# A Restormer block on one core: the first image's normalisation scaled on VectorE from PSUM, a shorter attention step, and a new order of the instructions

## The chip, the core and the metric

The kernel runs on one core of one Trainium2 chip, in fp32 throughout. The metric is the device time of one launch in microseconds, median of several runs. TensorE (PE), VectorE (DVE), ScalarE (ACT), GpSimd (POOL) and SyncE (SP) each take their own instructions strictly in the order in which the program holds them, and wait for each other through semaphores; DMA transfers are issued from the queues of SP and POOL (and at the start ACT).

## The reference, cut to what matters

```python
B, C, H, W = 16, 128, 96, 96; HEADS = 8; HID = 4 * C
xn1 = layernorm(x over C)                                  # LN1
q, k, v = xn1 @ wq.T, xn1 @ wk.T, xn1 @ wv.T               # per pixel
q, k = l2norm over the 9216 pixels, per channel
attn = softmax(einsum('bhcn,bhdn->bhcd', q, k) * D**-0.5)  # 16x16 for each of 8 heads
x = x + (attn @ v) @ wp.T
xn2 = layernorm(x over C)                                  # LN2
h1 = einsum('bchw,oc->bohw', xn2, w_in)                    # 128 -> 512 channels
h2 = depthwise 3x3 convolution of h1
x = x + einsum('bchw,oc->bohw', gelu(h2), w_out)           # 512 -> 128 channels
```

## The kernel before

**Tiling.** An image is 128 channels (the partitions) by 96 rows of 96 pixels. It is worked in 8 bands of 12 rows (1152 pixels), a band in 3 units of 4 rows (384 pixels). The hidden layer's 512 channels are 4 chunks of 128. A *job* is one chunk of one band; there are 128 bands.

**Stages of an image.** `norm(i, False)` is LN1: batches of 4 x 128 pixels are transposed by TensorE into PSUM (line 708), VectorE takes statistics (bn_stats, L716), POOL works out variance (L721) and its power -1/2 (L725), the batch is scaled, and TensorE adds the scaled batch to a 128x129 Gram matrix (L758) and transposes it back to the channels' layout (L808), from where ACT copies it into the ring `xn` (L814). In all images but the first, ACT copies the transposed batch from PSUM to the SBUF tile `zT` (L745), VectorE takes the statistics from there and POOL scales it in place (L751). In the first image the batch goes through the three PSUM banks `acc` that the taps use later; ACT copies it to SBUF (into tiles `h3` that are still free), and VectorE and POOL scale one half each (L751). `attention` turns the Gram matrix into one 128x128 matrix: L2 norms of q and k from the Gram matrix (L912 to L931, small 128x2 operations), the scores (L916 to L941), the exponential on ACT (L946, PSUM to SBUF), softmax on VectorE (L951 to L954), two more matmuls, and the matrix to SBUF (L971). `norm(i, True)` applies it (`mix`, L661), adds x (L667 on VectorE for the first bands of the first image, else L670 on ACT and a DMA that adds, L673), takes LN2's statistics from PSUM, and VectorE writes the scaled result to `xn` (`place`, L812).

**The feed-forward part.** For each job TensorE computes `hidden` (L1008) into one of four PSUM banks `h`, ACT copies it to SBUF (`kept`, L1013). The depthwise convolution's nine taps are split: VectorE does most of them as scalar_tensor_tensor operations on 128x1152 (below: *taps*; the first of a job takes POOL's `merged` as its addend, L1036 with acc as output; the middle ones L1040; the last one writes `h3`, L1036 with h as output). All middle and last taps of a job read the `acc` that the tap before them wrote. Two to four taps of a job are products made by ACT (L1024), brought in by POOL (`merge`, L1027, L1030) and by DMAs that POOL issues and that add in flight (L1049, L1052). ACT then takes the GELU (L1057). For one chunk in a third of the bands TensorE does the whole convolution instead (L1120). TensorE's `out` (L1161) sums the four chunks, and VectorE adds the result to x (`add`, L1168); SP stores it.

**What sets the order.** The functions do not issue instructions; they hand operations to a planner (`Plan`) with an engine, an assumed duration, what is read and written, and a place: a number of jobs from the operation's position in the work plus the entry of its kind in the table `AT` (entries `_0` are for the first image). `RANK` is added for the choice within an engine only, not for the turn in which buffers are given out. `Plan.order` plays the program through with the assumed durations; whenever an engine is free, the ready operation with the lowest place goes. The order of these starts is the order of the instructions in the program; at run time nothing is reordered.

Of the kernel before, what the change touches and what calls it, by code (L numbers as in the profile page):

```python
# [50 lines left out]
    load_w=-10696.6, weights=-1325.7, zeros=-1188.75, load_a=-32.75, forth_a=537.05, stats_a=22,  # L51
    variance_a=-862.55, power_a=-5924.95, pool_product=152.05, merge=-5342.4, scaled_a=-5192.6, gram=1195.35,
    back_a=409.4, place_a=886.65, attention=-25.55, mix=300.55, residual=204, mixed=1426, add_x=-865.9,
    forth_b=1131.25, stats_b=0.4, variance_b=-1458.9, power_b=-5365.35, shift_b=20.9, scaled_b=-3615.05,
    back_b=417.45, place_b=-1328.4, halo=2133.65, hidden=417.15, kept=888.55, products=-29.95, add_last=-5291.25,
    tap=11.15, add_first=-5453.25, gelu=2338.65, conv=1193.95, conv_gelu=10.7, out=420.9, add=-1325.35, store=7.1,
    mix_0=137.4, residual_0=1.6, mixed_0=28.95, add_x_0=-5926.95, gram_0=299.15, forth_a_0=-996.9, forth_b_0=321.4,
    stats_a_0=6.45, stats_b_0=-501.55, scaled_a_0=-863.8, copied_a=1384.75, copied_b=1870.85, copied_a_0=86.7,
    copied_b_0=1111, scaled_b_0=-128.2, back_a_0=299.35, back_b_0=412.9, place_a_0=137.4, place_b_0=-1368.1,
    shift_b_0=22.8, late=9.7,  # L60
)
RANK = dict(tap=-712.55, products=1729.15, forth_a=-347.95, forth_b=-713.5, conv_gelu=-713.7, mix=-53.4)
# [190 lines left out]
def tile_restormer_block(  # L253
# [92 lines left out]
    ccol = const.tile([P, 2, 2], F32, name="ccol")  # L346
    ncq = const.tile([1, P], F32, name="ncq")
    wqkT = const.tile([P, 2 * P], F32, name="wqkT")
    cqk = const.tile([1, 2 * P], F32, name="cqk")
# [98 lines left out]
    def move(p, f, r, w, ns, first=0):  # L448
        op("SP", 60 + first, p, f, r, w, 900 + SLACK, dma=ns)
# [15 lines left out]
    def weights(p):  # L465
# [4 lines left out]
        def loads():  # L470
            a, b = (flat(h3_bufs[plan.slot["h3", ("weights", k)]]) for k in range(2))
            v["win"] = a[:, :HID].rearrange("p (n c) -> p n c", c=P)
            v["wout"], v["wp"] = a[:, HID : 2 * HID], a[:, 2 * HID : 2 * HID + P]
            v["wqk"], v["wqkT"] = b[:, : 2 * P], b[:, 2 * P : 4 * P]
            v["wt"] = b[:, 4 * P : 8 * P].rearrange("p (t c) -> p t c", c=P)
            v["w1centre"], v["wvT"] = b[:, :P], b[:, P : 2 * P]
# [20 lines left out]
        def keep_qkp(pt):  # L497
            nc.vector.tensor_copy(v["wqkT"], pt[:, : 2 * P])
            nc.vector.tensor_scalar(wqkT, pt[:, : 2 * P], w1, None, ALU.mult)
            nc.vector.tensor_copy(wpT, pt[:, 2 * P : 3 * P])  # L500
            nc.vector.tensor_copy(v["wvT"], pt[:, 3 * P :])
            nc.vector.tensor_scalar(v["w1centre"], centre, w1, None, ALU.mult)
# [85 lines left out]
        pc = ("h", ("weights", "centred"))  # L588
        pe(1000, at("weights", p), centred, [("w", "qk"), mine[1]], [pc])
        dve(800, at("weights", p), keep_centred, [pc], [("w", "qk")])  # L590
# [54 lines left out]
    def norm(i, second, place_of):  # L645
# [41 lines left out]
        def pixels(s, m):  # L687
# [8 lines left out]
            by_dve = QT // 2 if early else 0  # L696
            apart = i == 0 and not second

# [11 lines left out]
            def stats(j):  # L710

                if j == 0:
                    d["st"] = small.tile([P, QB * QT // 2, 6], F32, tag="st", name=f"st_{name}_{m}")
                h, k = divmod(2 * j, QT)
                of = d["pT", qs[h]] if second or DIRECT else zT(qs[h])[:, :, :P]
                nc.vector.bn_stats(d["st"][:, j, :], of[:, k : k + 2, :].rearrange("p t c -> p c t"))  # L716
# [6 lines left out]
            def power():  # L723
                rstd = d["rstd"] = rstds[m] = small.tile([P, QB * QT], F32, tag="rstd", name=f"rstd_{name}_{m}")
                nc.gpsimd.tensor_tensor(rstd, d["ve"], mhalf, ALU.pow)  # L725
# [21 lines left out]
            def scaled(engine, q, ks):  # L747
                z = zT(q)[:, ks[0] : ks[-1] + 1, :P]
                t = (q - qs[0]) * QT
                rstd = d["rstd"][:, t + ks[0] : t + ks[-1] + 1]  # L750
                engine.tensor_tensor(z, z, rstd.unsqueeze(2).to_broadcast([P, len(ks), P]), ALU.mult)  # L751
# [12 lines left out]
            for q, tr in zip(qs, trs):  # L764
                units = {t // TPU: None for t in range(q * QT, (q + 1) * QT)}
                zt = zt_of(q)
                both = [(*zt, j) for j in range(2)]
                if apart and q % 2 == 0:
                    four = [(*zt_of(k), j) for k in (q, q + 1) for j in range(2)]
                    op("POOL", 200, at("zeros", s), lambda q=q: zT(q), [], four, 300)  # L770
                if second or DIRECT:
                    pe(112 * QT, at("forth" + ab, s, i), lambda q=q: forth(q), [xtok(u) for u in units], [tr])
                    continue
                pe(112 * QT, at("forth" + ab, s, i), lambda q=q: forth(q), [xtok(u) for u in units], [tr, both[0]])
                act(t_copy(QT * P), at("copied" + ab, s, i), lambda q=q: copied(q), [tr], both)
            for j in range(QB * QT // 2):
                of = trs[2 * j // QT] if second or DIRECT else (*zt_of(qs[2 * j // QT]), 0)
# [3 lines left out]
            for h, q in enumerate(qs if not second else ()):  # L781
                zt, sh = zt_of(q), s + STEP["scaled"] * h
                if DIRECT:
# [3 lines left out]
                if by_dve:  # L787
                    dve(by_dve * 150 + 60, at("scaled" + ab, sh, i), lambda q=q: scaled(nc.vector, q, range(by_dve)), [bt], [(*zt, 0)], True)
                pool((QT - by_dve) * T_SCALED + 100, at("scaled" + ab, sh, i), lambda q=q: scaled(nc.gpsimd, q, range(by_dve, QT)), [bt], [(*zt, 1)] if by_dve else [(*zt, 0), (*zt, 1)], True)
                if True:  # L790
                    pe(QT * 228, at("gram", sh, i), lambda q=q: gram(q), [(*zt, 0), (*zt, 1), ("w", "ones")], [("g", i)])
# [59 lines left out]
    def attention(s, i):  # L851


        places_of = dict(kq="ma", em="ma", y="ma", gs="mb", e="mb", a="mb")
        columns = dict(ps_u=0, ps_r=256, ps_c=256, ps_n=384, ps_kq=0, ps_qk=128, ps_y=256, ps_m=0, ps_d=384)
# [52 lines left out]
        def _():  # L908
            pn, pc = ps([P, 2], "ps_n"), ps([P, 2], "ps_c")
# [10 lines left out]
        @step("DVE", 670)  # L920
        def _():

            n2 = sb([P, 2], "n2")
            nc.vector.tensor_mul(n2, v["ps_c"], ccol[:, 0, :])
            nc.vector.tensor_add(n2, n2, ccol[:, 1, :])
            nc.vector.tensor_add(n2, v["ps_n"], n2)
            nc.vector.tensor_scalar(n2, n2, 1e-24, None, ALU.max)

        @step("POOL", 700)
        def _():  # L930
            nc.gpsimd.tensor_tensor(sb([P, 2], "rn"), v["n2"], mhalf[:, :2], ALU.pow)  # L931

        @step("DVE", 300)
        def _():
            nc.vector.tensor_scalar(sb([P, 1], "rq"), v["rn"][:, 0:1], float(D) ** -0.5, None, ALU.mult)

            nc.vector.tensor_scalar(sb([P, P], "kq"), v["ps_kq"], v["rn"][:, 1:2], None, ALU.mult)
# [6 lines left out]
        def _():  # L944

            nc.scalar.activation(sb([P, P], "e"), v["ps_qk"], AF.Exp, scale=v["rq"])  # L946

        @step("DVE", 1060)
        def _():
            em = sb([P, P], "em")  # L950
            nc.vector.tensor_mul(em, v["e"], blocks)  # L951
# [294 lines left out]
```

## Time and profile before

| | us |
|---|---|
| median of 3 runs (lowest to highest) | 4059.35 (4056.95 to 4065.53) |
| the profiled execution | 4061.62 |
| its span | 4059.9 |
| first tap starts / last tap starts | 107.11 / 4048.15 |

The page of the profile gives each engine's busy time, the groups of instructions by line with the mean time of one, and the idle time before them with what ended it. The windows of the trace give busy time by stretch, the timeline the start of each instruction. An operation's start to the next one's start on the same engine is the time that it really costs there, since ends overlap with the following start.

### The profile page before, as it was taken

Reading aid. Unit: us, or ns where it says so; the run is one execution under the profiler, and the core shown is the slowest. Engines: PE = TensorE matmul, PEld = TensorE weight load, DVE = VectorE, ACT = ScalarE, POOL = GpSimd, SP = SyncE. Lnnn points to the kernel's source line nnn. Section 1 sums busy time; section 2 is a strip of 40 time slices with the busy share of each in tenths; the row PEclk is TensorE's granted clock in tenths of the full one; section 3 lists DMA queues with packets and bytes.
Section 4 is the critical chain, followed back from the end, with each engine's and each line's share of the span. In section 5 each row is a group of like instructions: output and inputs, shape, how many; then the busy total and the mean of one; then the engine's idle time right before and its main releaser. Section 6 shows DMA issues by size and latency. Waiting matters only on the chain. (4 is left out here: it accounts for less than half of the span.)

```text
span 4059.9 us, 50967 instructions
## 1 busy us (share of the span) xinstructions
PE 3920.2 (97%) x16758; PEld 2516.4 (62%) x16758; DVE 3878.3 (96%) x4452; ACT 3579.4 (88%) x5204; POOL 3372.2 (83%) x3109
## 2 busy tenths in 40 slices
PE   8999999999999999999999999999999999999999
PEld 6656666666666666666666666666666566656555
DVE  6999999999999999999999999999999999999998
ACT  3989988999889888999989898989998989989886
POOL 6878978888888888888888888888888878888674
PEclk9999999999999999999999999999999999999999
DMA  2889999899998999999999999999999999999996
GB/s 90 168 185 202 203 202 194 185 204 201 192 200 185 193 196 195 202 202 202 193 198 211 192 194 188 211 189 205 198 193 193 197 196 202 195 205 185 185 189 143
DMA packets 191690, 777.41 MB, mean 191 GB/s; under 512 B 22208, under 2 KB 23616, under 8 KB 191424
## 3 DMA queue, kind: packets, MB, share of 16 engines
q0 software_dynamic: 151920, 622.33, 80.9%
q1 hardware_dynamic: 38256, 151.73, 10.1%
q8 instruction: 132, 2.16, 0.2%
q14 instruction: 134, 1.10, 0.1%
q10 hardware_dynamic: 1248, 0.09, 0.0%
HBM read 148.85 MB, written 75.50 MB: 55 GB/s over the span
## 5 line engine op out<-in xcount | busy, mean ns | idle before, releaser
L1024 ACT ACTIVATE pr<-h,ratio 128x1152 f32<-128x1152 f32 x1494 | 1826.5, 1269 | 32.5 <-DMA h<-pr 13.0
L1040 DVE SCALAR_TENSOR_TENSOR acc<-h,ratio,acc 128x1152 f32<-128x1152 f32 (+1 forms) x1308 | 1809.5, 1383 | 11.4
L1027 POOL TENSOR_TENSOR merged<-pr,h 128x1152 f32<-128x1152 f32 x466 | 1220.3, 2619 | 101.1 <-DVE acc L1036 61.0
L1008 PE MATMUL h<-xn,winT 128*128 128x384 f32 (+2 forms) x2802 | 1087.6, 496 | 21.0 <-ACT h L1013 8.3
L1161 PE MATMUL h<-h,woutT 128*128 128x384 f32 x3072 | 1072.1, 489 | 11.5 <-ACT h L1013 5.5
L1120 PE MATMUL h<-xn,comp 128*128 128x380 f32 (+2 forms) x2430 | 892.1, 484 | 4.7 <-ACT h L1013 2.0
L1013 ACT COPY h<-h 128x384 f32<-128x384 f32 (+2 forms) x1401 | 652.5, 492 | 198.2 <-PE h L1008 192.9
L1161 PEld LDWEIGHTS h<-h,woutT 128*128 128x128 f32 x3072 | 566.5, 190 | 377.4 <-ACT h L1013 13.6
L1036 DVE SCALAR_TENSOR_TENSOR acc<-h,ratio,merged 128x1152 f32<-128x1152 f32 x466 | 692.6, 1486 | 28.3 <-POOL merged L1030 9.1
L1052 POOL DMA_DIRECT2D h<-pr x466 | 455.6, 978 | 307.7 <-DVE h L1036 71.6
L1008 PEld LDWEIGHTS h<-xn,winT 128*128 128x128 f32 x2802 | 489.1, 190 | 301.6 <-issue 34.5
L1057 ACT ACTIVATE h<-h,ksum 128x1152 f32<-128x1152 f32 (+1 forms) x586 | 614.2, 1076 | 62.6 <-DMA h<-pr 61.3
L1036 DVE SCALAR_TENSOR_TENSOR h<-h,ratio,acc 128x1152 f32<-128x1152 f32 x467 | 654.9, 1402 | 11.1 <-PE h L1161 6.5
L1120 PEld LDWEIGHTS h<-xn,comp 128*128 128x128 f32 x2430 | 433.9, 190 | 246.0 <-issue 19.1
L1049 POOL DMA_DIRECT2D pr<-pr x466 | 466.5, 1005 | 107.7 <-ACT pr L1024 86.0
L708 PE MATMUL h<-ident,x 128*128 128x128 f32 x2212 | 322.7, 275 | 28.7 <-DMA x<-in_x_dram 9.6
L708 PEld LDWEIGHTS h<-ident,x 128*128 128x128 f32 x2212 | 262.5, 141 | 139.6 <-issue 48.6
L725 POOL TENSOR_TENSOR rstd_b<-ve_b,mhalf 128x4 f32<-128x4 f32 x288 | 334.7, 1167 | 14.5
L751 POOL TENSOR_TENSOR zT<-zT,rstd_a 128x512 f32<-128x512 f32 x270 | 333.5, 1238 | 8.7
L725 POOL TENSOR_TENSOR rstd_a<-ve_a,mhalf 128x4 f32<-128x4 f32 x288 | 309.1, 1074 | 16.9
L661 PE MATMUL h<-xn,mwT 128*128 128x384 f32 x768 | 289.8, 495 | 8.3 <-ACT x L670 2.5
L758 PEld LDWEIGHTS g<-zT 128*128 128x128 f32 x2160 | 271.0, 191 | 41.1 <-POOL zT L751 7.0
(189 smaller groups left out, 3977.1 us busy)
## 6 DMA issues: line engine op xcount, KB each, us to landing
pr<-pr POOLq DMA_DIRECT2D x466, 576.0 KB, 7.6
h<-pr POOLq DMA_DIRECT2D x466, 576.0 KB, 7.5
x<-in_x_dram SPq DMA_DIRECT2D x128, 576.0 KB, 7.5
out_dram<-x SPq DMA_DIRECT2D x127, 576.0 KB, 4.6
x<-in_x_dram POOLq DMA_DIRECT2D x123, 576.0 KB, 8.7
out_dram<-x SPq DMA_DIRECT2D x3, 192.0 KB, 1.9
h<-in_L_conv_w_in_dram SPq DMA_DIRECT2D x1, 256.0 KB, 3.4
h<-in_L_conv_w_out_dram SPq DMA_DIRECT2D x1, 256.0 KB, 3.7
```

Source lines behind the costliest of these rows:

```text
L708: nc.tensor.transpose(d["pT", q][:, k, :], xt[:, j * P : (j + 1) * P], ident)
L725: nc.gpsimd.tensor_tensor(rstd, d["ve"], mhalf, ALU.pow)
L1008: nc.tensor.matmul(rows(ph), lhsT=winT[:, n, :], rhs=window(xn, r0 + r, e - r, 1), start=True, stop=True)
L1013: nc.scalar.copy(window(h1_, r, e - r, 1), rows(d.pop(("ph", r))))
L1024: nc.scalar.activation(to, shifted(t), AF.Copy, scale=ratio[:, n, t : t + 1])
L1027: nc.gpsimd.tensor_tensor(merged, d["pr", dma_taps[0]], shifted(UNIT), ALU.add)
L1036: nc.vector.scalar_tensor_tensor(to, shifted(t), ratio[:, n, t : t + 1], also, ALU.mult, ALU.add)
L1040: nc.vector.scalar_tensor_tensor(to, shifted(t)[:, lo:hi, cut], ratio[:, n, t : t + 1], to, ALU.mult, ALU.add)
L1049: nc.gpsimd.dma_start(out=d["pr", dma_taps[1]], in_=d["pr", t], accum_op=ALU.add)
L1057: nc.scalar.activation(h3, h3, AF.Gelu, bias=ksum[:, z, n : n + 1])
L1120: nc.tensor.matmul(d["pc"][:, lo:hi, cut], lhsT=comp[:, t, :], rhs=window(xn, r0 + dy, UR, dx)[:, lo:hi, cut], start=(t == order[0]), stop ...
L1161: nc.tensor.matmul(rows(d["po"]), lhsT=woutT[:, n, :], rhs=h3s[g, n][:, s * UR : (s + 1) * UR, :], start=(k == 0), stop=(k == NCH - 1),)
```

## The change

1. **First image, LN1.** The batch stays in its `acc` bank. VectorE takes the statistics from PSUM and, when POOL has the power, scales the whole batch from PSUM into the SBUF tile (one operation of 128x4x128 instead of one of 128x2x128 on VectorE and one on POOL). ACT's copy is gone. The bank comes free after VectorE's scaling, not after ACT's copy.
2. **Attention, all images.** The factor that was applied to the linear part of the norms by VectorE is put into a new constant `wqk2c`, so that both parts of the norm are summed in PSUM; VectorE adds the constant part in one operation (four before). The maximum with 1e-24 moves to POOL. The factor D to the power -1/2 moves from an operation on `rq` into the scaling of `kq`. The exponential is written to PSUM and masked from there.
3. **The planner's numbers**: attention's assumed durations follow these edits, a load is assumed to land after 2000 instead of 900, and the tables `AT` and `RANK` are replaced.
4. The result of the power is written over its input (`ve`); a plain renaming in the rows below.

```diff
 AT = dict(
-    load_w=-10696.6, weights=-1325.7, zeros=-1188.75, load_a=-32.75, forth_a=537.05, stats_a=22,
...
+    load_w=-2305.35, weights=639.95, zeros=-342.95, load_a=-42.4, forth_a=-588.2, stats_a=1671.35,
...
-RANK = dict(tap=-712.55, products=1729.15, forth_a=-347.95, forth_b=-713.5, conv_gelu=-713.7, mix=-53.4)
+RANK = dict(tap=-1882.15, products=-1879.1, forth_a=-433, forth_b=-526, conv_gelu=-1389, mix=-1794.75)
...
-        op("SP", 60 + first, p, f, r, w, 900 + SLACK, dma=ns)
+        op("SP", 60 + first, p, f, r, w, (2000 if w else 900) + SLACK, dma=ns)
...
-            nc.vector.tensor_scalar(ccol[:, 0, :], c, 2.0, None, ALU.mult)
-            nc.vector.scalar_tensor_tensor(ccol[:, 1, :], c, NTOK / 2.0, ccol[:, 0, :], ALU.mult, ALU.mult)
+            nc.vector.tensor_scalar(ccol, c, 1.0, None, ALU.mult)
+            nc.vector.scalar_tensor_tensor(ccol, ccol, float(NTOK), ccol, ALU.mult, ALU.mult)
+            nc.vector.tensor_tensor(wqk2c, v["ptwos"], wqkT, ALU.mult)
...
-            by_dve = QT // 2 if early else 0
             apart = i == 0 and not second
+            from_psum = second or DIRECT or apart
...
-                if DIRECT:
+                if from_psum:
                     dve(605, at("scaled" + ab, sh, i), lambda q=q: direct(q), [bt, trs[h]], [(*zt, 0), (*zt, 1)])
...
-                if by_dve:
-                    dve(by_dve * 150 + 60, at("scaled" + ab, sh, i), lambda q=q: scaled(nc.vector, q, range(by_dve)), [bt], [(*zt, 0)], True)
...
-                nc.tensor.matmul(pc[:, z : z + 1], lhsT=wqkT[:, zs], rhs=v["s"], start=True, stop=True)
-                nc.tensor.matmul(pn[:, z : z + 1], lhsT=v["prod"][:, zs], rhs=ones, start=True, stop=True)
+                nc.tensor.matmul(pn[:, z : z + 1], lhsT=wqk2c[:, zs], rhs=v["s"], start=True, stop=False)
+                nc.tensor.matmul(pn[:, z : z + 1], lhsT=v["prod"][:, zs], rhs=ones, start=False, stop=True)
...
-            nc.vector.tensor_mul(n2, v["ps_c"], ccol[:, 0, :])
-            nc.vector.tensor_add(n2, n2, ccol[:, 1, :])
-            nc.vector.tensor_add(n2, v["ps_n"], n2)
-            nc.vector.tensor_scalar(n2, n2, 1e-24, None, ALU.max)
+            nc.vector.tensor_add(sb([P, 2], "n2"), v["ps_n"], ccol)
...
+            nc.gpsimd.tensor_scalar(n2, n2, 1e-24, 1.0, ALU.max, ALU.mult)
+            nc.gpsimd.tensor_tensor(sb([P, 2], "rn"), n2, mhalf[:, :2], ALU.pow)
...
-            nc.vector.tensor_scalar(sb([P, 1], "rq"), v["rn"][:, 0:1], float(D) ** -0.5, None, ALU.mult)
-            nc.vector.tensor_scalar(sb([P, P], "kq"), v["ps_kq"], v["rn"][:, 1:2], None, ALU.mult)
+            nc.vector.tensor_scalar(
+                sb([P, P], "kq"), v["ps_kq"], v["rn"][:, 1:2], float(D) ** -0.5, ALU.mult, ALU.mult
+            )
...
-            nc.scalar.activation(sb([P, P], "e"), v["ps_qk"], AF.Exp, scale=v["rq"])
+            nc.scalar.activation(ps([P, P], "ps_e"), v["ps_qk"], AF.Exp, scale=v["rn"][:, 0:1])
...
-            nc.vector.tensor_mul(em, v["e"], blocks)
+            nc.vector.tensor_mul(em, v["ps_e"], blocks)
```

**How the order moves, at three places.** Line numbers of the changed kernel are about 2 to 8 higher (taps L1036 and L1040 become L1038 and L1042, add L1168 becomes L1170, place L812 becomes L816, statistics L716 become L724). Numbers at the end of a name are those of buffers.

The first place is VectorE in the middle of the first image's LN1 (h_... are SBUF tiles that hold batches, `st_a` the statistics of image 0). Before:

```order
L716 BN_STATS st_a_9_392<-h_6_160 128x6
L751 TENSOR_TENSOR h_4_158<-h_4_158,rstd_a_4_375 128x2x128
L716 BN_STATS st_a_9_392<-h_6_160 128x6
L716 BN_STATS st_a_10_414<-h_7_161 128x6
L716 BN_STATS st_a_11_422<-h_7_161 128x6
L716 BN_STATS st_a_10_414<-h_7_161 128x6
L551 COPY h_1_155<-h_73 128x512
L552 TENSOR_SCALAR winT<-h_73,w_99 128x512
L751 TENSOR_TENSOR h_4_158<-h_4_158,rstd_a_5_420 128x2x128
L751 TENSOR_TENSOR h_5_159<-h_5_159,rstd_a_6_434 128x2x128
```

And now, read from `acc`, whole batches:

```order
L724 BN_STATS st_a_6_342<-acc 128x6
L737 TENSOR_TENSOR h_4_159<-acc,ve_a_5_344 128x4x128
L724 BN_STATS st_a_7_371<-acc 128x6 x2
L737 TENSOR_TENSOR h_5_160<-acc,ve_a_6_363 128x4x128
L724 BN_STATS st_a_8_386<-acc 128x6 x2
L737 TENSOR_TENSOR h_5_160<-acc,ve_a_7_383 128x4x128
```

Before, statistics ran up to seven batches ahead of the scaling and the preparation of weights (L551, L552 and others) stood among them; now each scaling stands one or two batches behind its statistics, and most weight preparation comes after the Gram matrix is complete.

The second place is TensorE in the first image's attention, from the transposition of the scores (L941, now L943) to the matmul with the softmax's result (L958, now L960). `x_1`, `x_2`, `x_3` are bands of the second image. Before:

```order
L941 MATMUL h_75<-ident,kq_856 128x128
L708 MATMUL h_74<-ident,x_1_531 128x128 x2
L708 MATMUL h_74<-ident,x_2_836 128x128 x2
L708 MATMUL h_73<-ident,x_2_836 128x128 x4
L708 MATMUL h_76<-ident,x_2_836 128x128 x3
L708 MATMUL h_76<-ident,x_3_869 128x128
L958 MATMUL h_75<-wpT,a_879 128x128
```

Now, with weight preparation (L493, L576) between them:

```order
L943 MATMUL h_73<-ident,kq_725 128x128
L493 MATMUL h_76<-ident,h_1_156 128x128 x4
L716 MATMUL h_74<-ident,x_0_536 128x128
L716 MATMUL h_74<-ident,x_1_702 128x128 x3
L716 MATMUL h_75<-ident,x_1_702 128x128 x4
L576 MATMUL h_76<-comp,centre 128x512
L493 MATMUL h_74<-ident,h_1_156 128x128 x4
L960 MATMUL h_73<-wpT,a_766 128x128
```

The second image's batches have moved back (8 transpositions less stand before this attention), and the weights stand in the gaps of the attention. In the whole program TensorE has 233 matmuls ahead of the first matmul of this attention (271 in the kernel before) and 392 ahead of the first `hidden` (441).

The third place is VectorE in the middle of the program, around the norms of image 8's attention (`n_8`); the rows with `ratio` are taps. Before:

```order
L1040 SCALAR_TENSOR_TENSOR acc<-h_2_143,ratio,acc 128x1152
L924 TENSOR_TENSOR n_8_13284<-g_11959,ccol 128x2
L925 TENSOR_TENSOR n_8_13284<-n_8_13284,ccol 128x2
L926 TENSOR_TENSOR n_8_13284<-g_11959,n_8_13284 128x2
L927 TENSOR_SCALAR n_8_13284<-n_8_13284 128x2
L1036 SCALAR_TENSOR_TENSOR h_4_158<-h_2_143,ratio,acc 128x1152
L1168 TENSOR_TENSOR x_7_3_12374<-h_73,x_7_3_12374 128x384
L1036 SCALAR_TENSOR_TENSOR acc<-h_3_144,ratio,merged 128x1152
L935 TENSOR_SCALAR rq_13305<-rn_13293 128x1
L937 TENSOR_SCALAR kq_13307<-g_11959,rn_13293 128x128
```

And now:

```order
L1042 SCALAR_TENSOR_TENSOR acc<-h_2_144,ratio,acc 128x1152
L927 TENSOR_TENSOR n_8_12874<-g_11477,ccol 128x2
L1042 SCALAR_TENSOR_TENSOR acc<-h_2_144,ratio,acc 128x1152
L724 BN_STATS st_a_1_12882<-zT_164 128x6
L1042 SCALAR_TENSOR_TENSOR acc<-h_2_144,ratio,acc 128x1152
L1170 TENSOR_TENSOR x_7_3_12008<-h_73,x_7_3_12008 128x384
L1038 SCALAR_TENSOR_TENSOR h_1_156<-h_2_144,ratio,acc 128x1152
L937 TENSOR_SCALAR kq_12904<-g_11477,rn_12888 128x128
L1038 SCALAR_TENSOR_TENSOR acc<-h_3_145,ratio,merged 128x1152
```

Six small operations have become two, and single operations stand alternately with taps. Over the whole program a tap stands directly behind another tap in 390 places (549 in the kernel before); behind the first tap, two or more other operations stand between two taps in 45 places (210).

More of the change, by code (lines that the diff above doesn't have):

```diff
@@ L723, in power @@
             def power():
-                rstd = d["rstd"] = rstds[m] = small.tile([P, QB * QT], F32, tag="rstd", name=f"rstd_{name}_{m}")
-                nc.gpsimd.tensor_tensor(rstd, d["ve"], mhalf, ALU.pow)
+                rstd = d["rstd"] = rstds[m] = d["ve"]
+                nc.gpsimd.tensor_tensor(rstd, rstd, mhalf, ALU.pow)
             def direct(q):
@@ L770, in pixels @@
                     op("POOL", 200, at("zeros", s), lambda q=q: zT(q), [], four, 300)
-                if second or DIRECT:
-                    pe(112 * QT, at("forth" + ab, s, i), lambda q=q: forth(q), [xtok(u) for u in units], [tr])
+                if from_psum:
+                    to = [tr] if second or apart else [tr, both[0]]
+                    pe(112 * QT, at("forth" + ab, s, i), lambda q=q: forth(q), [xtok(u) for u in units], to)
                     continue
```

67 lines of the change are left out of this document (35 added, 32 removed).

## The prediction, made before the changed kernel ran

> **What bounds the kernel now.** First the page's totals:
>
> ```profile
> PE 3920.2 (97%) x16758; PEld 2516.4 (62%) x16758; DVE 3878.3 (96%) x4452; ACT 3579.4 (88%) x5204; POOL 3372.2 (83%) x3109
> ```
>
> Two engines are full, PE and DVE. A share over the whole span doesn't tell which one gives way, so I cut the span at the first and the last tap (the timeline of DVE) and ask for busy time by window. Columns: sum and mean of PE, PEld, DVE, ACT, POOL, then granted clock, DMA share, GB/s.
>
> ```profile
> 107.11 2.19 DVE L1036 SCALAR_TENSOR_TENSOR acc<-h,ratio,merged 128x1152 f32<-128x1152 f32 x1 [1.58 <-POOL merged L1027]
> 4048.15 1.42 DVE L1036 SCALAR_TENSOR_TENSOR h<-h,ratio,acc 128x1152 f32<-128x1152 f32 x1
> 0.00:107.10 107.10, 89.60 (x608) 73.53 (x609) 65.49 (x197) 38.75 (x80) 70.32 (x141) 0.97 0.26 86
> 107.10:4048.10 3941.00, 3822.37 (x16128) 2438.51 (x16126) 3809.67 (x4251) 3538.12 (x5119) 3301.85 (x2969) 1.00 0.93 195
> 4048.10:4059.90 11.80, 8.21 (x25) 4.33 (x24) 3.10 (x5) 2.54 (x6) 0.00 (x0) 1.00 0.14 50
> ```
>
> So time = start 107.1 + tap stretch 3941.0 + tail 11.8. In the stretch DVE is idle for 131 us (3.3%), PE for 119, at a granted clock of 1.00, and the DMA engines are at 0.93. The waits of DVE tell whom it lacks (columns: us in total, times, longest):
>
> ```profile
> DVE x L1168 <- PE h L1161: 37.4, 46, 2.9
> DVE xn L812 <- PE h L808: 20.5, 27, 1.7
> DVE st_a L716 <- ACT zT L745: 13.0, 11, 2.6
> DVE acc L1036 <- POOL merged L1030: 9.1, 13, 1.8
> DVE st_b L716 <- PE h L708: 8.9, 12, 2.6
> ```
>
> There is no large wait. PE's busy time contains pauses between queued matmuls, while DVE's operations follow each other back to back; PE's sums also wait for the taps, four chunks at a time. I take DVE as what sets the stretch: a microsecond less there shortens it by nearly one, as long as PE and the transfers follow. That is my main choice.
>
> **The change part by part.** The taps, their products, additions and transfers are the same in number; what differs is small operations and order.
>
> *Attention on VectorE.* The groups of one operation each (count | busy, mean ns | idle before), then the spread (min/median/max ns) of three of them, and the POOL group behind the spread:
>
> ```profile
> L924 DVE TENSOR_TENSOR n<-g,ccol 128x2 f32<-128x2 f32 x15 | 2.2, 145 | 0.0
> L925 DVE TENSOR_TENSOR n<-n,ccol 128x2 f32<-128x2 f32 x16 | 13.9, 870 | 0.5
> L926 DVE TENSOR_TENSOR n<-g,n 128x2 f32<-128x2 f32 x15 | 2.4, 159 | 0.5
> L927 DVE TENSOR_SCALAR n<-n 128x2 f32<-128x2 f32 x16 | 7.5, 466 | 0.6
> L935 DVE TENSOR_SCALAR rq<-rn 128x1 f32<-128x1 f32 x16 | 2.3, 146 | 0.8 <-POOL rn L931 0.8
> L937 DVE TENSOR_SCALAR kq<-g,rn 128x128 f32<-128x128 f32 x15 | 5.1, 339 | 0.0
> L951 DVE TENSOR_TENSOR em<-e,blocks 128x128 f32<-128x128 f32 x16 | 13.1, 818 | 2.3 <-ACT e L946 2.3
> L954 DVE TENSOR_SCALAR a<-em,rden 128x128 f32<-128x128 f32 x16 | 8.2, 512 | 0.6
> L925 DVE TENSOR_TENSOR n<-n,ccol x16: 160/578/3058, 63.0 to 3750.1; 128x2 f32<-128x2 f32 x16
> L927 DVE TENSOR_SCALAR n<-n x16: 169/169/2499, 63.4 to 3750.5; 128x2 f32<-128x2 f32 x16
> L951 DVE TENSOR_TENSOR em<-e,blocks x16: 274/288/2814, 66.3 to 3764.6; 128x128 f32<-128x128 f32 x16
> L1027 POOL TENSOR_TENSOR merged<-pr,h 128x1152 f32<-128x1152 f32 x466 | 1220.3, 2619 | 101.1 <-DVE acc L1036 61.0 <-ACT pr L1024 30.7 <-ACT h L1013 4.5
> ```
>
> The operations that read only SBUF (L925, L927, L951, L954) are sometimes held for up to 3 us, about one merge of POOL; those that read PSUM (L924, L926, L937) keep their 0.15 to 0.34. The change removes L924, L925, L927, L935, keeps one addition from PSUM (price of L926, as before), and lets L951 read PSUM, which I price at L937, same shape from PSUM. Saved per image: 0.145 + 0.870 + 0.466 + 0.146 + (0.818 - 0.339) = 2.11 us; 15 attentions lie in the stretch: **-31.6**. Lower bound: the holds merely move to the next operation, and only the smallest durations go, 0.145 + 0.160 + 0.169 + 0.146 = 0.62, times 15 = -9.3 (reading PSUM then gains nothing, 0.288 against 0.339). I take the means: the rows show holds at these operations, while L924 and L926, next to them, show none. ACT's exponential into PSUM and POOL's added maximum lie on engines with 12% and 17% free. The maximum takes about L721's 0.52 (below), the removed operations about as much, so the attention's own chain stays as long: nothing.
>
> [...]
>
> *The order on VectorE.* A tap behind another tap waits for it (it reads its `acc`). Timeline of DVE, start and duration ("x2" is two in a row):
>
> ```profile
> 2040.11 2.87 DVE L1040 SCALAR_TENSOR_TENSOR acc<-h,ratio,acc 128x1152 f32<-128x1152 f32 x2
> 2042.89 0.42 DVE L716 BATCH_NORM_STATS2 st_a<-zT 128x6 f32<-128x256 f32 x1
> 2043.23 1.40 DVE L1040 SCALAR_TENSOR_TENSOR acc<-h,ratio,acc 128x1152 f32<-128x1152 f32 x1
> 2044.54 0.42 DVE L716 BATCH_NORM_STATS2 st_a<-zT 128x6 f32<-128x256 f32 x1
> ```
>
> Two taps take 2042.89 - 2040.11 = 2.78, so the first of them takes 2.78 - 1.31 = 1.47 up to the next tap's start; a tap before a small operation takes 2044.54 - 2043.23 = 1.31. So a direct pair costs about 0.15 more. The rows of the order give 549 such pairs before, 390 now: 159 x 0.15 = **-24**. Bounds: 0, if the operation that now stands between pays the gap itself, and -24; I take -24, since these rows show the statistics following without it.
>
> [...]
>
> *The start.* PE's transpositions of the second image and preparations that stood ahead of the first attention have moved back. The places in the timeline:
>
> ```profile
> 27.49 1.04 PE L708 MATMUL acc<-ident,x 128*128 128x128 f32 x8
> 57.13 0.27 ACT L879 COPY gs<-g 128x129 f32<-128x129 f32 x1 [0.36 <-PE g L758]
> 99.85 2.33 PE L1008 MATMUL h<-xn,winT 128*128 128x480 f32 x6
> L708 PE MATMUL h<-ident,x 128*128 128x128 f32 x2212 | 322.7, 275 | 28.7 <-DMA x<-in_x_dram 9.6
> ```
>
> LN1 ends at 57.1, the first `hidden` comes at 99.9, the first tap at 107.1. Of 441 matmuls ahead of the first `hidden` 392 remain; 49 at 1.04 / 8 = 0.13 are 6.4. In the attention itself PE now has five matmuls more between L943 and L960, 0.65 if nothing there waits. Bounds: +0.65 (only these five count, the rest was covered by waits) to -12 (44 net at the group's mean of 0.275); I take **-6**, by the row of this stage.
>
> *Is VectorE too slow for the first image's banks?* A bank of three is now held until VectorE has scaled the batch:
>
> ```profile
> L716 DVE BATCH_NORM_STATS2 st_a<-h 128x6 f32<-128x256 f32 x36 | 13.5, 414 | 0.4 <-ACT h L745 0.4
> L721 POOL TENSOR_SCALAR ve_a<-st_a 128x4 f32<-128x4 f32 x288 | 146.3, 520 | 44.2 <-DVE st_a L716 43.9
> L725 POOL TENSOR_TENSOR rstd_a<-ve_a,mhalf 128x4 f32<-128x4 f32 x288 | 309.1, 1074 | 16.9
> L812 DVE TENSOR_TENSOR xn<-x,h 128x384 f32<-128x384 f32 x384 | 206.4, 547 | 25.3 <-PE h L808 20.5 <-ACT h L1013 1.1 <-ACT pr L1024 1.0
> L606 DVE COPY woutT<-h 128x512 f32<-128x512 f32 x1 | 0.7, 669 | 0.0
> 8.66 1.94 PE L708 MATMUL acc<-ident,x 128*128 128x128 f32 x8 [8.66 <-DMA x<-in_x_dram]
> ```
>
> Two statistics 0.83, variance 0.52, power 1.07, and the scaling, not in the trace: above L812's 0.55 with fewer elements, I take L606's 0.67. That is 3.1 us a bank; with three banks (`acc`) one batch each 1.03 us, while 18 batches between 8.7 and 57.1 come every 2.7 us by the loads. VectorE's own part, 1.5 us a batch, fits too. Both costs are covered by the loads; if they were not, 18 x 1.03 = 18.5 would still be below the 48 available. Nothing. On the other hand eight statistics of the second image, ahead of the first tap before, now lie in the stretch, at 0.34 from start to start (2043.23 - 2042.89): **+2.7**.
>
> *What is late next.* The stretch gets 31.6 + 24 - 2.7 = 53 us (1.3%) shorter, and PE, ACT and the DMA engines must do the same work in it. The DMA share of 0.93 becomes 0.943, so free DMA time falls by a fifth; PE's idle 119 us would fall to 66, by 45%. The waits of DVE, 89 us in the five rows above, won't shrink by themselves. If they grow about as much as PE's idle time falls, by 40%, that is +35; at least 0. I take the middle, **+18**.
>
> Sum: -31.6 - 24 - 6 + 2.7 + 18 = -41. The profiled execution took 4061.6 (its span 4059.9 and 1.7 around it), so 4020.7; it was 2.3 above the median of the runs, so **4018**.
>
> **The rivals.**
>
> *Better:* the waits don't grow and the start gives its 12: 4018 - 18 - 6 = 3994. For it: all engines have over 2% idle. Against: 0.93 on the DMA engines.
>
> *The alternation is worth nothing:* 4018 + 24 = 4042. For it: only a few dozen starts were read in the timeline. [...]
>
> *The holds move to the next operation:* 31.6 - 9.3 = 22 back: 4040.
>
> *The change doesn't do what it says,* VectorE doesn't set the stretch. PE is as busy (3822 against 3810) and both kernels have the same matmuls; then the stretch stays 3941 and only the start counts: 4059.3 - 6 = 4053.
>
> *Slower: an operation that waits for PE stops the taps.* VectorE takes its instructions in turn; with single operations alternating with taps, an addition (L1170) whose sum isn't ready holds the next tap, and behind it POOL's merge and PE's next sum. A wait costs 37.4 / 46 = 0.81. Two thirds of the bands, 85, have all four chunks on VectorE; one more wait in each is 85 x 0.81 = +69: 4018 + 69 = 4087. It undoes the gain from 41 / 0.81 = 51 new waits, and shows as slower from about 60. For it: waits on PE are already the largest rows. Against: an addition had single taps around it in most places before, too.
>
> **How the numbers follow.** Forecast (4005 to 4036) 0.47; better 0.13; alternation nothing 0.08; holds move 0.08; VectorE not the bound 0.10; slower 0.14. The range goes from below the better case, 3990 (it could win another 4 by fewer waits), to just above the 4053, 4056: outside are the slower case and a small part of the better one. A measurement of this kernel tells about 0.2%, 8 us, from no change. Faster than 4051.2: 0.47 + 0.13 + 0.08 + 0.08 = 0.76; the same 0.10; slower than 4067.5: 0.14.
>
> **What would show it.** Right: DVE's busy time in the stretch falls by some 50 us; n2's addition stays near 0.16 and em near 0.34 without a maximum near 3; tap to next start 1.31 in about 160 more places; the first tap near 101; DVE's waits on PE grow by less than 35. Wrong: the stretch keeps 3941 with DVE's idle time grown by what its busy time lost (VectorE was not the bound), waits of L1170 and L816 in over 100 places (slower), em's holds found again at L954's successor, or a first image whose `acc` waits for VectorE's scaling (L737) so that the Gram matrix ends after 57.

## The result, and the profile after

| | before | after |
|---|---|---|
| median (lowest to highest), us | 4059.93 (4056.95 to 4065.53) | 4014.02 (4013.62 to 4020.85) |
| ratio, 95% interval | | 0.9889 (0.9872 to 0.9906) |
| profiled execution / its span | 4061.62 / 4059.9 | 4020.85 / 4019.1 |

The change gains 1.1%, some 45 us. The forecast was 4018. The sum came out, but not the choice that it stands on: VectorE doesn't set the pace. The sections below show both. The profiled execution of the changed kernel was the slowest of its four, 6.8 us above their median (1.7 before), so the profiles show 41 us of the 45.

The totals of the page, and the windows of the trace cut at the first and the last tap (columns as before: length; busy time of PE, PEld, DVE, ACT, POOL; clock, DMA share, GB/s):

```profile
PE 3908.1 (97%) x16760; PEld 2525.4 (63%) x16760; DVE 3834.9 (95%) x4390; ACT 3562.0 (89%) x5186; POOL 3378.7 (84%) x3107
0.00:110.34 110.34, 88.18 (x556) 69.92 (x557) 67.82 (x186) 22.35 (x50) 50.84 (x113) 1.00 0.22 72
110.34:4007.40 3897.06, 3812.38 (x16184) 2451.64 (x16183) 3763.96 (x4201) 3537.74 (x5133) 3327.91 (x2995) 1.00 0.94 197
4007.40:4019.10 11.70, 7.51 (x23) 3.89 (x21) 3.08 (x4) 1.88 (x5) 0.00 (x0) 1.00 0.14 50
```

The tap stretch is 3941.0 - 3897.1 = 44 us shorter, the start 3 longer, the tail the same. In the stretch VectorE's busy time fell by 45.7 and its idle time stayed (131.3 before, 133.1 now). That reads exactly as forecast: a full engine got less to do. But another pair of numbers stands beside it: TensorE's idle time in the stretch fell from 118.6 to 84.7, and its busy time by 10, with 56 rows of matmuls more in it. One profile can't tell which engine led; it took loads put on each of them.

The attention's operations on VectorE after the change, by form, and the spread (min/median/max):

```profile
L927 DVE TENSOR_TENSOR n<-g,ccol 128x2 f32<-128x2 f32 x15 | 2.2, 145 | 0.0
L937 DVE TENSOR_SCALAR kq<-g,rn 128x128 f32<-128x128 f32 x15 | 5.2, 345 | 0.0
L953 DVE TENSOR_TENSOR em<-g,blocks 128x128 f32<-128x128 f32 x15 | 4.2, 282 | 0.0
L956 DVE TENSOR_SCALAR a<-em,rden 128x128 f32<-128x128 f32 x16 | 10.6, 662 | 0.6
L953 DVE TENSOR_TENSOR em<-g,blocks x15: 276/282/285, 249.8 to 3703.1; 128x128 f32<-128x128 f32 x15
L956 DVE TENSOR_SCALAR a<-em,rden x16: 285/288/2034, 76.4 to 3704.0; 128x128 f32<-128x128 f32 x16
```

What reads PSUM is not held: the mask (em), now read from there, takes 276 to 285 ns, where it went up to 2814. Part of the hold has moved to `a`, which reads only SBUF: 662 on average, 512 before. The two operations between them, `den` and `rden`, read only SBUF too and are not held (286 and 164 ns on average, before and after).

TensorE's own waits, which the prediction doesn't show. Of before, then of after (us in total, times, longest):

```profile
PE h L808 <- POOL rstd_b L725: 14.9, 14, 2.6
PE h L708 <- DMA x<-in_x_dram: 9.6, 10, 2.2
PE acc L708 <- DMA x<-in_x_dram: 8.7, 1, 8.7
PE h L1008 <- ACT h L1013: 8.3, 10, 2.6
PE g L958 <- DVE a L954: 7.3, 7, 2.2
```

```profile
PE h L1010 <- ACT h L1015: 11.6, 14, 3.3
PE h L812 <- POOL ve_b L733: 9.1, 11, 1.6
PE h L1122 <- ACT h L1015: 6.0, 8, 1.9
PE acc L716 <- DVE st_a L724: 5.5, 12, 1.0
PE h L716 <- DMA x<-in_x_dram: 1.5, 3, 0.8
```

The ten waits for loaded images (9.6 us) became three (1.5), those for the LN2 power (`rstd_b`, now `ve_b`) fell from 14.9 to 9.1. There is also a new one: in the first image TensorE waits twelve times for VectorE before it fills an `acc` bank (L716 <- `st_a`).

### The profile page after: what moved, and what is told of

It reads as the page before. It is cut to its first block, busy times and chain, and to the rows that moved or that the text cites. A ratio compares the mean times of both kernels' runs of the same rounds, so it can differ in the third digit from the quotient of the medians.

```text
span 4019.1 us, 50885 instructions
## 1 busy us (share of the span) xinstructions
PE 3908.1 (97%) x16760; PEld 2525.4 (63%) x16760; DVE 3834.9 (95%) x4390; ACT 3562.0 (89%) x5186; POOL 3378.7 (84%) x3107
## 4 chain that ended last, share of the span: by engine, by line
PE 55%; DVE 14%; ACT 9%; DMA 9%; POOL 8%; issue 5%; POOLq 0%; DVEq 0%; ACTq 0%
PE h L1163 15%; PE h L1010 13%; PE h L1122 12%; DVE acc L1042 6%; DMA h<-pr 5%; ACT pr L1026 5%; PE h L669 4%; PE h L812 4%; PE g L764 3%; PE h L716 3%; DVE acc L1038 2%; DVE h L1038 2%; POOL merged L1029 2%; ACT h L1015 2%; DMA pr<-pr 2%
## 5 line engine op out<-in xcount | busy, mean ns | idle before, releaser
L1042 DVE SCALAR_TENSOR_TENSOR acc<-h,ratio,acc 128x1152 f32<-128x1152 f32 (+1 forms) x1308 | 1810.4, 1384 | 8.1
L1029 POOL TENSOR_TENSOR merged<-pr,h 128x1152 f32<-128x1152 f32 x466 | 1239.7, 2660 | 97.8 <-ACT pr L1026 48.9
L1163 PE MATMUL h<-h,woutT 128*128 128x384 f32 x3072 | 1090.3, 489 | 4.2 <-ACT h L1015 2.1
L1010 PEld LDWEIGHTS h<-xn,winT 128*128 128x128 f32 x2802 | 500.1, 190 | 339.1 <-issue 36.2
L1038 DVE SCALAR_TENSOR_TENSOR acc<-h,ratio,merged 128x1152 f32<-128x1152 f32 x466 | 685.9, 1472 | 26.0 <-POOL merged L1032 12.6
L1054 POOL DMA_DIRECT2D h<-pr x466 | 475.1, 1019 | 244.3 <-DVE h L1038 38.4
L1038 DVE SCALAR_TENSOR_TENSOR h<-h,ratio,acc 128x1152 f32<-128x1152 f32 x467 | 655.1, 1403 | 5.3 <-PE h L1163 2.0
L1051 POOL DMA_DIRECT2D pr<-pr x466 | 489.0, 1058 | 109.5 <-ACT pr L1026 80.3
L733 POOL TENSOR_TENSOR ve_b<-ve_b,mhalf 128x4 f32<-128x4 f32 x288 | 379.2, 1317 | 7.7
L757 POOL TENSOR_TENSOR zT<-zT,ve_a 128x512 f32<-128x512 f32 x270 | 338.3, 1257 | 5.7
L733 POOL TENSOR_TENSOR ve_a<-ve_a,mhalf 128x4 f32<-128x4 f32 x288 | 321.5, 1118 | 15.6
L716 PE MATMUL h<-ident,x 128*128 128x128 f32 x2212 | 310.9, 274 | 16.3 <-DVE st_b L724 4.5
L716 PEld LDWEIGHTS h<-ident,x 128*128 128x128 f32 x2212 | 258.9, 141 | 99.1 <-issue 38.1
```

Source lines behind the costliest of these rows:

```text
L716: nc.tensor.transpose(d["pT", q][:, k, :], xt[:, j * P : (j + 1) * P], ident)
L733: nc.gpsimd.tensor_tensor(rstd, rstd, mhalf, ALU.pow)
L1010: nc.tensor.matmul(rows(ph), lhsT=winT[:, n, :], rhs=window(xn, r0 + r, e - r, 1), start=True, stop=True)
L1029: nc.gpsimd.tensor_tensor(merged, d["pr", dma_taps[0]], shifted(UNIT), ALU.add)
L1038: nc.vector.scalar_tensor_tensor(to, shifted(t), ratio[:, n, t : t + 1], also, ALU.mult, ALU.add)
L1042: nc.vector.scalar_tensor_tensor(to, shifted(t)[:, lo:hi, cut], ratio[:, n, t : t + 1], to, ALU.mult, ALU.add)
```

## The experiments

Two questions: which part of the change gained how much, and which engine sets the pace. All ratios are to the kernel before, timed beside it; the changed kernel stands at 0.9889. A difference between two experiments is uncertain by some 5 to 12 us.

### The attention alone, in the old and in the new order

Inside the planner's steps only the instructions were exchanged; the steps' durations and thus the order stayed. In the old order:

```diff
-            nc.vector.tensor_mul(n2, v["ps_c"], ccol[:, 0, :])
-            nc.vector.tensor_add(n2, n2, ccol[:, 1, :])
-            nc.vector.tensor_add(n2, v["ps_n"], n2)
-            nc.vector.tensor_scalar(n2, n2, 1e-24, None, ALU.max)
+            nc.vector.tensor_add(sb([P, 2], "n2"), v["ps_n"], ccol)
...
+            nc.gpsimd.tensor_scalar(n2, n2, 1e-24, 1.0, ALU.max, ALU.mult)
...
-            nc.scalar.activation(sb([P, P], "e"), v["ps_qk"], AF.Exp, scale=v["rq"])
+            nc.scalar.activation(ps([P, P], "ps_e"), v["ps_qk"], AF.Exp, scale=v["rn"][:, 0:1])
```

> The kernel before with only the attention's instructions changed; every step stands where it stood. (The linear part of the norms is multiplied by zero here instead of its factor, and the planner's durations stay old, so that the order doesn't move.) Theory, VectorE sets the pace and the holds of 128x2 and SBUF-only operations vanish with them: 30 us less, 4030, ratio 0.9925. Rival, holds move on to the next operation: 9 us less, 4050, ratio 0.998. Rival, VectorE doesn't set the pace: 4060, ratio 1.000.

Measured: ratio 0.9977 (0.9968 to 0.9986), 9 us less; 4051.7. The operations from `n` to `a`, sixteen of each, took 62.5 us of VectorE before and 33.1 here, about what the forecast counted, and VectorE's busy time in the stretch fell by 23 us (3809.7 to 3786.4). So the holds did not all move on; yet the time fell by 9 only. The number is the one that the rival gave, for another reason. The row of `a` in this kernel shows how much of the hold moved:

```profile
L954 DVE TENSOR_SCALAR a<-em,rden 128x128 f32<-128x128 f32 x16 | 13.4, 840 | 0.6
```

In the new order, the reverse edit (the old instructions put back):

> The changed kernel with the old attention instructions put into the same steps, so that the new order stays. Theory: 30 us more than the changed kernel's 4014, 4044, ratio 0.996. Rival, holds move: 4023, ratio 0.991. Rival, VectorE doesn't set the pace, the order alone made the gain: 4014, ratio 0.989.

Measured: ratio 0.9946 (0.9934 to 0.9958), 4039.84; 23 us slower than the changed kernel. So the order (with the first image's LN1) is worth some 22 us by itself, all of it in the tap stretch (3941.0 to 3916.5). The attention is worth 23 us on top of it, though only 9 in the old order; that difference is little more than its uncertainty. TensorE's waits, summed by who ended them, suggest why the same edit differs: in the old order those for VectorE fell by 12 us (34.2 to 22.3) while those for POOL rose by 6 (21.3 to 27.1); in the new order those for VectorE fell by 21 (52.5 to 31.2) and those for POOL stayed (8.6 to 9.1). That is read from the traces, not tried separately.

### Pairs of taps, made and unmade

First the old order with fewer pairs: where two or more other operations follow each other on VectorE and a direct pair of taps comes behind them, the taps between move up by one place each.

```diff
-        return [ops[k][3] for k in sorted(range(len(ops)), key=lambda k: (starts[k], k))]
+        seq = sorted(range(len(ops)), key=lambda k: (starts[k], k))
+        return [ops[k][3] for k in swaps(self, seq)]
```

> The kernel before with nothing changed but this: where two or more other operations follow each other on VectorE and a direct pair of taps comes behind them, the taps between move up by one place each, which leaves 429 direct pairs of taps instead of 549. Theory, a pair costs 0.15 more than a tap before another operation: 120 x 0.15 = 18 us less, 4042, ratio 0.9956. Rival, the alternation is worth nothing: 4060, ratio 1.000. Rival, the operations that are moved behind a tap are late for whom they serve: slower than 4060.

Measured: ratio 1.0155 (1.0141 to 1.0169), 63 us slower, with 120 pairs less. What came is the prediction's slower rival: waits of VectorE for TensorE, and, which that rival didn't name, of TensorE for VectorE (34.2 us in all before, 88.4 here).

```profile
DVE x L1199 <- PE h L1192: 58.7, 67, 3.2
DVE xn L843 <- PE h L839: 39.3, 50, 5.8
```

```profile
PE h L1039 <- DVE xn L843: 16.7, 21, 2.8
PE h L839 <- POOL rstd_b L756: 12.9, 13, 2.6
PE h L1039 <- DVE x L1199: 10.2, 17, 1.3
PE h L692 <- DVE st_b L747: 9.5, 10, 1.9
```

TensorE's next `hidden` (L1039 here) stands behind an addition or a `place` that came one tap later and still held its PSUM bank. Here the alternation was worth less than the lateness that it brought.

Then the new order with more pairs (the same hook; a tap goes ahead of statistics that stand alone between two taps):

> The changed kernel with direct pairs of taps made on purpose: where statistics stand alone between two taps, the second tap goes ahead of them; 894 direct pairs instead of 390. Theory: 504 x 0.15 = 76 us more than 4014, 4090, ratio 1.0075. Rival, a pair costs nothing: 4014, ratio 0.989; then the start of a tap to that of the next is 1.32 also for these pairs, or the statistics behind take 0.15 less.

Measured: ratio 1.0067 (1.0055 to 1.0079), 4089.26; the forecast by the price of a pair was 4090. Agreement to a microsecond, and still no proof. A tap before a tap does cost more: 1.45 us to the next start, as before, and the statistics behind keep their 0.34. But TensorE's waits tell of another cost:

```profile
PE h L689 <- DVE st_b L744: 28.0, 31, 1.8
PE h L1030 <- DVE st_b L744: 18.5, 20, 1.9
PE h L832 <- DVE st_b L744: 13.4, 12, 2.0
PE h L736 <- DVE st_b L744: 8.4, 7, 2.5
```

In these rows TensorE waits 68 us for the statistics of LN2 (`st_b`), 72.5 over all rows; in the changed kernel it is 11. The statistics read PSUM, and the bank comes free one tap later. So the same swaps were made for one norm at a time.

> The changed kernel with 256 direct pairs of taps more (646 instead of 390), made only where the statistics between two taps are those of LN2, which hold a PSUM bank that TensorE needs again. If pairs cost by VectorE's time: 256 x 0.15 = 38, 4052, ratio 0.998. If they cost because TensorE waits for the bank (71 us of such waits with all 504 pairs): +60 to 70, 4079, ratio 1.005.

> The changed kernel with 283 direct pairs of taps more (673 instead of 390), made only where the statistics between two taps are those of LN1, which read SBUF and hold no PSUM bank. If pairs cost by VectorE's time: 283 x 0.15 = 42, 4056, ratio 0.999. If only TensorE's waits count: +0 to 10, 4019, ratio 0.990.

```diff
+        if is_tap(w) and "stats" in kind(x) and ops[x][3].__defaults__[1] is True and is_tap(t) and not is_tap(u) and not ops[t][5] and x not in ops[t][4] and all(pos[d] < pos[x] for d in ops[t][4]):
+            before[x] = t
```

(`w`, `x`, `t`, `u` follow each other on VectorE; `__defaults__[1]` is True for statistics of the second norm, and for the run on the first norm the line asks for False.) Measured: 1.0000 (0.9991 to 1.0009) for LN2's statistics, 45 us slower than the changed kernel with 256 pairs; 0.9940 (0.9927 to 0.9952) for LN1's, 21 us slower with 283 pairs. By VectorE's time alone the two would be 38 and 42. A pair that delays a bank cost over twice what another did (0.18 against 0.07), and TensorE's waits are of the kind seen above:

```profile
PE h L689 <- DVE st_b L744: 20.3, 24, 1.9
PE h L1030 <- DVE st_b L744: 16.1, 18, 1.5
PE h L832 <- DVE st_b L744: 9.0, 10, 1.9
PE h L736 <- DVE st_b L744: 8.1, 6, 2.9
```

Neither expectation held to the number: 45 is below the 60 to 70 and not far from the 38, and 21 is above the 0 to 10 and half of the 42. So the number for LN2 alone doesn't part the two causes; the two runs side by side and the waits do. TensorE's waits for `st_b` grew from 11 to 57 us in the run for LN2, as much as was lost, and to 13 in the other. What the 21 consist of stays open; in that run TensorE's waits for VectorE rose by 10 us in all (31.2 to 40.7) and those for POOL by 3.5.

### A load on each engine

One more statistics operation per band on VectorE, or one more matmul per band on TensorE, in both orders:

```diff
+    spare = const.tile([P, 6], F32, name="spare")
...
             nc.vector.tensor_add(xt, d["po"], xt)
+            if s == 1:
+                nc.vector.bn_stats(spare, wqkT)
```

```diff
                 d["po"] = bank(("out", g, s), UT)
+                if s == 1:
+                    nc.tensor.matmul(
+                        rows(d["po"]), lhsT=woutT[:, n, :], rhs=h3s[g, n][:, s * UR : (s + 1) * UR, :], start=True, stop=True
+                    )
```

> The changed kernel with one more statistics operation (128x256 from a constant in SBUF, result unused) behind the middle addition of each band: 128 x 0.34 = 44 us of VectorE. Theory, VectorE alone sets the pace of the new order: +44, 4058, ratio 0.9997. Rival, TensorE sets it as much: some +20, 4034, ratio 0.994; TensorE alone: 4014, ratio 0.989.

> The changed kernel with the first matmul of the middle sum of each band done twice (128x384): 128 x 0.33 = 42 us of TensorE. Theory, VectorE alone sets the pace: at most +10, 4024, ratio 0.991. Rival, TensorE sets it as much: +20 or more, 4034, ratio 0.994; TensorE alone: +42, 4056.

> The kernel before with the same 44 us more on VectorE. The attention's edit alone took 23 us of VectorE's time from this order and gave only 9.5 us; if VectorE and TensorE share the pace here, an addition also shows in part only: +20, 4080, ratio 1.005. Theory, VectorE alone sets the pace, and a gain was lost for another reason: +44, 4104, ratio 1.011.

> The kernel before with the same 42 us more on TensorE. If the two engines share the pace in the old order and not in the new one: +20 or more here, 4080, ratio 1.005, and less than half of it in the new order. If TensorE doesn't set the pace in either: at most +10 in both.

How large were the loads? The operation on VectorE takes 0.34 us to the next start, 128 x 0.34 = 44 us. The matmul is twice what the expectations count: in this trace a matmul of 384 columns shows as two rows, 256 for 128 matmuls, and rows that follow each other start 0.32 us apart, (3.39 - 0.49) / 9. So TensorE's load is 256 x 0.32 = 83 us, not 42; with it TensorE's busy time in the stretch rose by 69 (from 3812) and its idle time fell by 28 (from 84.7 to 56.8).

```profile
L1164 PE MATMUL h<-h,woutT x256: 483/486/590, 162.1 to 4051.2; 128*128 128x384 f32 x128
2010.97 3.39 PE L1163 MATMUL h<-h,woutT 128*128 128x384 f32 x10
109.56:4047.98 3938.42, 3881.64 (x16438) 2501.50 (x16437) 3768.81 (x4200) 3547.62 (x5133) 3319.03 (x2995) 1.00 0.94 195
```

| | ratio (interval) | against the kernel it was made from |
|---|---|---|
| VectorE +44, new order | 0.9907 (0.9884 to 0.9930) | +7 |
| TensorE +83, new order | 0.9995 (0.9983 to 1.0007) | +43 |
| VectorE +44, old order | 1.0016 (1.0003 to 1.0029) | +6.5 |
| TensorE +83, old order | 1.0091 (1.0072 to 1.0110) | +37 |

About half of TensorE's load shows, and a sixth of VectorE's, in both orders. That the 43 is the 42 of an expectation is chance, as the load was twice that. The extra matmul also makes the sum for VectorE's addition later; what is due to that and what to TensorE's time these runs don't part. VectorE's waits for the sums, of the new order, first without a load, then with the one on TensorE:

```profile
DVE x L1170 <- PE h L1163: 43.7, 41, 3.8
```

```profile
DVE x L1174 <- PE h L1167: 83.3, 90, 4.3
```

### Work taken from each engine

> The changed kernel without the first of the four matmuls of the middle sum of each band (one hidden chunk is missing in a third of the output): 128 x 0.33 = 42 us less of TensorE. If TensorE sets the pace: -42, 3972, ratio 0.979. If VectorE does: 4014, ratio 0.989.

```diff
             if k == 0:
                 d["po"] = bank(("out", g, s), UT)
+                if s == 1:
+                    return
...
-                start=(k == 0), stop=(k == NCH - 1),
+                start=(k == (s == 1)), stop=(k == NCH - 1),
```

> The changed kernel with every statistics operation reading 128 values a row instead of 256 (the variance is then of half the channels): about 0.13 less each, 1100 x 0.13 = 147 us less of VectorE. If VectorE sets the pace: at least -100, 3914 or below, ratio 0.964. If TensorE does, only what it waits for VectorE can go, 31 us at most with its knock-on: 3985 to 4010, ratio 0.982 to 0.988.

```diff
-                nc.vector.bn_stats(d["st"][:, j, :], of[:, k : k + 2, :].rearrange("p t c -> p c t"))
+                nc.vector.bn_stats(d["st"][:, j, :], of[:, k : k + 2, : P // 2].rearrange("p t c -> p c t"))
```

Measured: 0.9852 (0.9837 to 0.9866) without the matmuls, 15 us less for 83 us of work (two rows each, as above), neither the 0 nor the 42 that were expected; 0.9881 (0.9864 to 0.9898) with the short statistics, 3 us less, which can't be told from nothing. The windows and VectorE's waits of the second:

```profile
106.96:3998.85 3891.89, 3812.31 (x16184) 2450.93 (x16183) 3638.10 (x4200) 3539.84 (x5133) 3351.18 (x2995) 1.00 0.95 198
```

```profile
DVE x L1170 <- PE h L1163: 80.5, 88, 4.4
DVE xn L816 <- PE h L812: 58.4, 94, 2.6
```

VectorE is 126 us less busy in the stretch (3764.0 to 3638.1) and the stretch is 5 us shorter: what it saved, it waits. Its waits grew by 119 us over the whole program, those for TensorE by 86 and those for ScalarE by 23. TensorE's busy time is the same, 3812. This settles that VectorE's time is not what the changed kernel is short of.

For TensorE it is not so clear: work added to it shows to a half, work taken from it to less than a fifth. The chain of work that ended last, from the page (followed back from the last instruction, at each step to what released it, as far as semaphores tell), has a share of every engine. Of the changed kernel, of the one with more matmuls, the one with fewer, and the one with short statistics:

```profile
PE 55%; DVE 14%; ACT 9%; DMA 9%; POOL 8%; issue 5%; POOLq 0%; DVEq 0%; ACTq 0%
PE 74%; DVE 8%; ACT 7%; POOL 4%; DMA 4%; issue 3%; POOLq 0%; DVEq 0%; ACTq 0%
PE 39%; DVE 23%; DMA 11%; ACT 10%; POOL 10%; issue 6%; POOLq 0%; DVEq 0%; ACTq 0%
PE 59%; ACT 12%; DMA 9%; POOL 9%; DVE 7%; issue 5%; POOLq 0%; ACTq 0%; DVEq 0%
```

TensorE has the largest share in all four, over half in three. With work taken from it its share falls to 39% and the others' rise. ScalarE, POOL and the DMA engines (0.94 busy in the stretch) were not loaded, so how much each of them counts stays open. In the kernel before, the chain of the page covers only a fifth of the span and tells little.

## Why the prediction was right, point by point

**What bounds the kernel: wrong.** "I take DVE as what sets the stretch" was the main choice. VectorE's time isn't what is short: 44 us more of it cost 6.5 and 7, and in the changed kernel 126 us less gave nothing that can be told. TensorE's time counts for more, but doesn't set the pace alone: 83 us more cost 37 and 43, 83 us less gave 15. The reason given, that TensorE's busy time contains pauses and VectorE's operations stand back to back, doesn't decide it; idle shares of 3.0% and 3.3% couldn't. The rival "VectorE doesn't set the stretch" was right in that, but its 4053 took the stretch as fixed. It isn't: TensorE's waits fell by 27 us over the whole program (127.7 to 100.7, the sum over the rows of its list), 12 of them for POOL and 9.5 for loads; those for VectorE fell by 3 only.

**Attention, -31.6: 9 in the old order, 23 in the new.** That reads from PSUM are not held was right (em 285 at most, n 145). What it saves on VectorE was right too: 29 us in the old order (62.5 to 33.1). That the rest stays unheld was not: `a` took over 5.2 us in the old order. And a microsecond of VectorE's time isn't one of the kernel's: here 29 were worth 9. In the new order the edit was worth nearly what it saved; TensorE's waits for VectorE fell by 21 there, but whether they are the cause was not tried.

**Order, -24 for 159 pairs: about 22 together with LN1, but not shown to be for the pairs.** The price on VectorE is real: a median of 1.46 (before) and 1.45 (after) from tap to tap and 1.32 from tap to another operation. The Trainium skill, in "VectorE: DVE Perf Modes", section "The DRAIN you can't avoid", says that the next operation does not start until the pipe is empty, and that one which is not held starts earlier. The rows go with both: behind a tap of 1.4 us an operation that doesn't need it starts after 1.32, the next tap after 1.46. But unmaking 120 pairs cost 63 us, and making 504 cost 72. LN2's pairs cost 45; at the 0.07 that LN1's cost they would have cost 19, so some 26 are an estimate of what the banks that came free later added. The same 0.07 makes 12 of the 159 pairs, half of the -24, if nothing else moved; what gave the rest of the 22 stays open.

**The start, -6: +3 in the profiled execution, +1 on average.** In the executions whose start holds the same instructions, the first tap stood at 107.1 to 109.0 (mean 108.1, four of the old start) and at 107.2 to 110.9 (mean 109.5, seven of the new one). The banks: "Nothing" was wrong. The forecast counted a bank's own steps, 3.1 us by three banks. On VectorE, though, the scaling of one batch stands between the statistics of the next two, and each waits for what comes before it in the line:

```profile
28.91 0.66 PE L716 MATMUL acc<-ident,x 128*128 128x128 f32 x4 [0.59 <-DVE st_a L724]
31.02 0.66 PE L716 MATMUL acc<-ident,x 128*128 128x128 f32 x4 [0.56 <-DVE st_a L724]
33.46 0.66 PE L716 MATMUL acc<-ident,x 128*128 128x128 f32 x4 [0.23 <-DVE st_a L724]
62.14 0.27 ACT L883 COPY gs<-g 128x129 f32<-128x129 f32 x1 [1.15 <-PE g L764]
```

A batch takes 2.1 to 2.4 us in these rows, not 1.03, and LN1 ends at 62.1 instead of 57.1; the shorter way from there to the first tap makes up for a third of that. Most of these 5 us come from a late load. VectorE's first operation on the weights of the depthwise convolution (`dw`) waits for them, before and after:

```profile
9.06 0.17 DVE L535 TENSOR_SCALAR unit<-dw 128x4 f32<-128x4 f32 x1 [8.01 <-DMA dw<-in_L_conv_w_dw_dram]
13.44 0.17 DVE L538 TENSOR_SCALAR unit<-dw 128x4 f32<-128x4 f32 x1 [12.39 <-DMA dw<-in_L_conv_w_dw_dram]
```

In the new start the end of LN1 follows this operation: it comes 48.1 to 48.7 us behind it in all seven executions, wherever it stands (11.0 to 14.1), and 45.5 behind it with the short statistics. So VectorE's line sets LN1 there, and 4.4 of the 5 us are the weights'. In the old start it doesn't follow (44.8 to 50.0 behind). The forecast saw no loss here, as it took the loads of the images for the limit. Whether the new order makes these weights late was not tried.

**Give-back, +18: +2.** VectorE's idle time in the stretch hardly changed: VectorE's time was not the limit, and TensorE's idle time fell as well.

So the sum fits by cancellation, which is luck: the attention gave 9 us less than the term (23 for 31.6) and the start 7 to 9 less, while the give-back of 18 didn't come; the order gave about what was put down, but by the estimate above only half of it for the reason given. The range held for reasons that the forecast didn't have.

## What to carry to other kernels

When two engines are both over 95% busy, the profile doesn't tell which one leads; put a small load on each (one operation per band), read its size from the trace of the loaded kernel, and see how much of it shows in the time. Then take work away as well: it may show that no engine leads alone. Don't count what an edit on an engine is worth by the time saved there; look at who waits for it, above all at when a shared PSUM bank comes free. And a forecast that an experiment confirms to the microsecond can still rest on the wrong cause: split the experiment so that the two causes part.

## What the runs showed of the hardware that was not expected

A hold of VectorE's SBUF-only operations does not fall on all of them (`den` and `rden` took at most 290 and 167 ns in all fourteen kernels), and it moves with the line-up: with the same instructions `a` averaged 840 ns in the old order and 640 to 716 in five kernels of the new one, while its shortest was 285; with the mask reading PSUM, at most 297 in nine kernels, nothing was ever added there. And 126 us less work on VectorE, 3% of the span, changed the time by less than can be measured while its share still read 92%: here a share above 90% was no sign of a bound.
